# Column lists made tile by tile, 130 listed blocks for 146, and hub edge sums moved to the third layer, in a four-layer graph kernel

## The chip, the cores and the metric

The kernel runs as one program on one core of a Trainium2 chip. The time is device microseconds of one execution. The kernel before took 2622.95 us, the median of 3 runs (2618.31 to 2624.23).

## What is computed

`x` is 4096 x 256, `adj` is 4096 x 4096 in float32, with a full diagonal and otherwise few entries, many of them in the first rows and columns, few in the late ones. Four layers each add their result to `x` and normalize each row:

```python
x = layernorm(x + adj @ (x * W))                       # layer 0
x = layernorm(x + L1(x, adj, W1, W2, W3, U1, U2))       # layer 1: two steps of top-p attention and of R = (adj + I) / rowsum
x = layernorm(x + softmax_of_edges(adj, x @ H_v) @ x)   # layer 2
x = layernorm(x + [x, adj @ x, edge] @ weight + bias)   # layer 3, edge[i] = sum_j adj[i, j] * adj[j, i]
```

## The kernel before, in words

The 4096 rows are 32 tiles of 128. `adj` is cut into 32 x 32 blocks of 128 x 128. The first `DENSE` = 3 tiles of rows (the hubs) use all 32 blocks of columns in every layer. A later tile needs only the columns in which one of its rows has an entry, and these are listed: the list holds `CAPS[I]` blocks of 128 column numbers, and one block is fetched with an indirect DMA on GpSimd (`gather`, L393), which takes one index for each partition. Two index tables are kept, `idx_x` for rows of a feature table and `idx_a` for rows of the packed adjacency. `CAPS` sums to 146 over the 29 listed tiles.

**Layer 0** is a hand-written loop (L620 to L641, under `manual_schedule`, so the order of the loop is the order on PE, ACT, DVE and POOL). One round of it takes one step of several generators:

- `dense_0` (L544): tiles 0 to 15, one panel of four blocks in a round (128 rounds): a 256 KB load on SP's queue, four matmuls, and a maximum over the panel on DVE (L552) that writes into `seen` which columns have entries.
- `find_0` (L555): tiles 16 to 31 are not multiplied densely. One 512 KB load in a round, and a DVE maximum (L563); 64 rounds, so it ends halfway through the dense tiles.
- `list_columns(1)` (L319), only after `find_0` is done: the lists of tiles 16 to 31 all at once. Ten rounds of `max` and `match_replace` on DVE (L347, L349) take out eight entries each; then small matmuls and DVE steps turn them into indices.
- `listed_0` (L566), after that, one started every third round: gathers of a tile's blocks and of its rows of `x` (L393), matmuls (L593), the sum of products with the transposed block (`edge`, L595, L402, L598), a write of the gathered blocks to HBM (`packed`, L602).
- `edges_0` (L604), from the same point on: the edge sums of the three hub tiles. Two 2 MB loads of `hubs` for each tile on ACT's queue (L608) into the two `e` buffers, and two products of 2048 columns on DVE (L614).
- `list_columns(0)`: the lists of tiles 3 to 15; three steps of it at the end of layer 0, the rest beside layer 1.
- `out_0` (L477): the end of a tile, in seven steps in successive rounds: scale, normalize (with a power on POOL, L492), transpose (L245), two projections (L294, L297), a product with 512 columns (L464), copies on ACT (L299 to L304, L511), `qp` on DVE (L516), and seven stores on ACT's queue.

**Layer 1, first attention step** (L1361 on): each tile is cut into named pieces (`AT`) with times, `PERIOD` = 15.8 us apart, and the pieces of all tiles are sorted by due time. `r_stream` fetches the listed blocks of tiles 16 to 31 and 3 to 15 at evenly spaced times beside them. The remaining steps of `list_columns(0)` are further events in the first three periods. The constants that build a list from marks (`before`, `up_to`, `next_one`, `step_up`, `slots`, `slot_1`, `ranks`; L1095 to L1115) are made here. `r_dense` (L1457) then handles the three hubs, and the second attention step follows, one tile in some 32 us.

**Layers 2 and 3** are `product` (L1612) with n = 0 and n = 1. Their chunks are hub panels (`HUBS` = 3 tiles densely in layer 2, 6 in layer 3) and pieces of lists of up to five blocks, in an order with a lead of 5 and 12 hub chunks. For each kind four chunks are fetched ahead. In layer 2 each block is weighted before its matmul: an exponential on ACT (L1593), a mask on DVE (L1594); a finished tile goes through `out_2`. Layer 3's gathers read what `out_2` has stored.

Of the kernel before, what the change touches and what calls it, by code (L numbers as in the profile page):

```python
# [47 lines left out]
L_EVERY, L_WAIT = 3, 5  # L48
HB = 8
# [12 lines left out]
NL = 8  # L62
NG = 2
LE = P // NL
DENSE = 3
CAPS = (NT,) * DENSE + (7, 7, 6, 7, 5, 6, 5, 5, 5, 5, 5, 5, 6) + (5,) * 8 + (4,) * 8
PIECE = 5

# [6 lines left out]
def gnn_kernel(ctx: ExitStack, tc: tile.TileContext, x, pair, panels, W0, W1, W2T, W3T, U1T, U2T,  # L75
# [41 lines left out]
    enter(loads=6, gat=16, tmp=1, w0=2)  # L117
# [53 lines left out]
    iota16 = iota([LE], "iota16", [[1, LE]])  # L171
    place = iota([512], "place", [[1, 512]], base=1, pool=pools["tmp"])
# [3 lines left out]
    def bits(op, v, name):  # L176

        i = small.tile([P, 1], I32, name="bits")
        nc.vector.tensor_scalar(i, row, v, None, op0=op)
        t = const.tile([P, 1], F32, name=name)  # L180
        nc.vector.tensor_copy(t, i)
        return t

    def equal(iot, v, n, name, dtype=F32):
        t = const.tile([P, n], dtype, name=name)
        nc.vector.tensor_scalar(t, iot, v, None, op0=OP.is_equal)
        return t

    row_list = equal(iota8, bits(OP.bitwise_and, NL - 1, "r7"), NL, "row_list")
    row_place = equal(iota16, bits(OP.arith_shift_right, 3, "r3"), LE, "row_place", BF16)  # L190
    slot_list = bits(OP.arith_shift_right, 4, "slot_list")
    slot_is = equal(iota8, slot_list, NL, "slot_is")
    slot_tile = equal(iota16, bits(OP.bitwise_and, 15, "r15"), LE, "slot_tile")

# [117 lines left out]
    deepest = max(CAPS[DENSE:LE]), max(CAPS[LE:])  # L312
    first_col = [0, LE * deepest[0]]
    n_cols = first_col[1] + LE * deepest[1]
    idx_x = const.tile([P, n_cols], I32, name="idx_x")
    idx_a = const.tile([P, n_cols], I32, name="idx_a")
    over = const.tile([1, NG], F32, name="over")

    def list_columns(g, apart=False):  # L319

        K = deepest[g]
        n = K * LE
        own = tmp_tile([P, NT, NL, LE], BF16)
        some = pools["tmp"].tile([P, NT, LE], BF16, name="some")
        nc.vector.tensor_scalar(some, seen[:, :, g * LE:(g + 1) * LE], 0.0, None, op0=OP.is_gt)
        for s in range(NL):
            nc.vector.tensor_scalar(own[:, :, s, :], some, row_list[:, s:s + 1], None, op0=OP.mult)
        yield  # L330
        ps = bank([P, NT, LE], "psl", "tp")
        for J in range(NT):
            nc.tensor.matmul(ps[:, J, :], own[:, J].rearrange("p a b -> p (a b)"), row_place, start=True, stop=True)
        yield
        left = pools["lists"].tile([P, 512], F32, name="left")
        flat = ps.rearrange("p a b -> p (a b)")
        free = pools["lists"].tile([P, 512], F32, name="free")
        nc.vector.scalar_tensor_tensor(free, flat, 0.5, place, op0=OP.is_lt, op1=OP.mult)
        spare = one("spare")
        nc.vector.tensor_reduce(spare, free, AX.X, OP.max)  # L340
        count = one("count")
        nc.vector.tensor_reduce(count, flat, AX.X, OP.add)
        nc.vector.scalar_tensor_tensor(left, flat, 0.5, place, op0=OP.is_gt, op1=OP.mult)
        found = pools["lists"].tile([P, LE * max(deepest)], F32, name="found")
        for r in range(n // 8):
            t8 = found[:, r * 8:(r + 1) * 8]
            nc.vector.max(t8, left)  # L347
            if r < n // 8 - 1:
                nc.vector.match_replace(left, t8, left, 0.0)  # L349
            yield  # L350
        pad = free[:, :n]
        nc.vector.tensor_scalar(pad, found[:, :n], 0.0, spare, op0=OP.is_equal, op1=OP.mult)
        nc.vector.tensor_tensor(found[:, :n], found[:, :n], pad, op=OP.add)
        psi = bank([P, K, LE], "psi", "tp")
        for k in range(K):
            sel = pools["lists"].tile([P, NL, LE], F32, name="sel", bufs=2)
            fk = found[:, k * LE:(k + 1) * LE]
            nc.vector.tensor_tensor(sel, slot_is.unsqueeze(2).to_broadcast([P, NL, LE]),
                                    fk.unsqueeze(1).to_broadcast([P, NL, LE]), op=OP.mult)
            nc.tensor.matmul(psi[:, k, :], sel.rearrange("p a b -> p (a b)"), slot_tile, start=True, stop=True)  # L360
        if apart:
            yield

        cols = slice(first_col[g], first_col[g] + K * LE)
        j = free[:, :n]
        nc.vector.tensor_scalar(j, psi.rearrange("p a b -> p (a b)"), float(NL), slot_list, op0=OP.mult, op1=OP.add)
        nc.vector.tensor_scalar(j, j, float(-NL), None, op0=OP.add)
        nc.vector.tensor_copy(idx_x[:, cols], j)
        at = iota([K, LE], "at", [[0, K], [1, LE]], base=g * LE, pool=pools["lists"])
        nc.vector.scalar_tensor_tensor(idx_a[:, cols], j, float(NT), at.rearrange("p a b -> p (a b)"),  # L370
                                       op0=OP.mult, op1=OP.add)

        pst = bank([P, P], "pst", "tp")
        nc.tensor.matmul(pst[:1, :], count, ident, start=True, stop=True)
        room = pools["lists"].tile([1, NL, LE], F32, name="room")
        for i in range(LE):
            nc.gpsimd.memset(room[:, :, i:i + 1], float(CAPS[g * LE + i] * LE))
        rm = room.rearrange("p a b -> p (a b)")
        nc.vector.tensor_tensor(rm, pst[:1, :], rm, op=OP.is_gt)
        nc.vector.tensor_reduce(over[:, g:g + 1], rm, AX.X, OP.max)  # L380
# [7 lines left out]
    def col(I, k):  # L388
        c = first_col[I // LE] + k * LE + I % LE
        return slice(c, c + 1)  # L390
# [76 lines left out]
    def find_columns(J):  # L467

        for u in range(2 * J, 2 * J + 2):
            b, h = LE + u % LE, u // LE  # L470
            t = pools["loads"].tile([P, HB, P], F32, name="half", bufs=2)
            nc.sync.dma_start(t.rearrange("p (c k) i -> p c (k i)", k=JC),
                              panels[b, h * HB // JC:(h + 1) * HB // JC].rearrange("c p k i -> p c (k i)"))
            nc.vector.tensor_reduce(seen[:, h * HB:(h + 1) * HB, b], t, AX.X, OP.max, apply_absolute_value=True)

# [57 lines left out]
    def move_ends():  # L533

        far = done
        for e in ends:
            if far - e[1] >= 2:
                e[1] = e[1] + 1 if next(e[0], e) is not e else done
            far = e[1]
        while ends and ends[0][1] == done:  # L540
            ends.pop(0)
# [13 lines left out]
    def find_0():  # L555
        for b in range(LE, NT):
            e = pools["e"].tile([P, N], F32, name="e")
            for h in range(NT // HB):
                t = e[:, h * HB * P:(h + 1) * HB * P]
                nc.sync.dma_start(t.rearrange("p (c x) -> p c x", x=JC * P),  # L560
                                  panels[b, h * HB // JC:(h + 1) * HB // JC].rearrange("c p k i -> p c (k i)"))
                yield
                nc.vector.tensor_reduce(seen[:, h * HB:(h + 1) * HB, b], t.rearrange("p (t i) -> p t i", i=P), AX.X,  # L563
                                        OP.max, apply_absolute_value=True)
# [39 lines left out]
    def edges_0():  # L604
        for I in range(DENSE):
            pair_of = [pools["e"].tile([P, N], F32, name="e") for _ in range(2)]
            for t, src in zip(pair_of, hubs):
                nc.scalar.dma_start(t, src[rows(I), :])  # L608
            for _ in range(6):
                yield  # L610
            part = small.tile([P, 2], F32, name="part_e")
            for h in range(2):
                a, b = (t[:, h * (N // 2):(h + 1) * (N // 2)] for t in pair_of)
                nc.vector.scalar_tensor_tensor(a, a, 1.0, b, op0=OP.mult, op1=OP.mult, accum_out=part[:, h:h + 1])  # L614
                yield
            nc.vector.tensor_add(edge[:, I:I + 1], part[:, 0:1], part[:, 1:2])

    everything = {getattr(mybir.EngineType, k) for k in ("PE", "Activation", "DVE", "Pool")}
    with tc.manual_schedule(engines=everything):
        sums_of_edges = edges_0()  # L620
        dense = (step for I in range(LE) for step in dense_0(I))
        find, lists, others = find_0(), list_columns(1, True), None
        left, active, n, heads = list(range(LE, NT)), [], 0, 3
        while heads or ends or active or left:
            move_ends()
# [766 lines left out]
    def r_stream(blocks):  # L1392
        due, t = [], 0
        for b in blocks:
            if b == DENSE:
                run(lists)
# [458 lines left out]
```

## Time and profile before

| | us |
|---|---|
| median of the runs | 2622.95 |
| profiled execution, its own time | 2627.68 |
| its span, from the first to the last instruction | 2625.9 |
| first matmul of layer 1 (end of layer 0) | 503.8 |
| first and last `mid` (one for each tile) of the first attention step | 521.5 and 1023.9 |
| last store of layer 1, first gather of layer 2 | 2240.0, 2242.7 |
| first and last gather of layer 3 | 2455.1, 2613.8 |

PE is busy for 2197.5 us (84%), DVE 2064.5 (79%), POOL 1704.6 (65%), ACT 1478.7 (56%). The mean granted clock of TensorE is 0.933. In answers by stretch, each row gives the length, each engine's busy time and instructions, the granted clock, the share of time in which the 16 DMA engines were busy, and what they moved. In lines of the timeline the bracket is the idle time before the instruction and what ended it. In lines of waits the numbers are us in total, times, and the longest. Neither an engine's own share nor a wait says by itself what a stage is bound by: it is read from who waits last in that stage.

### The profile page before, as it was taken

How to read it: one execution, taken by the hardware profiler on the slowest of the kernel's cores; microseconds unless marked ns; L12 is line 12 of the kernel's file. 1: busy time of each engine (PE TensorE's matmuls, PEld its weight loads, DVE VectorE, ACT ScalarE, POOL GpSimd, SP SyncE). 2: the span in 40 equal slices, each digit the busy share in tenths (PEclk: the TensorE clock that was granted, in tenths of full speed). 3: DMA queues.
4: the chain of work that ended last, by engine and by line, in shares of the span. 5: the costliest groups of instructions: out<-in, count | busy, mean ns of one | idle time of the engine just before them, and what ended most of it. 6: DMA issues, size and time to landing. Idle time of an engine off the chain costs nothing.

```text
span 2625.9 us, 37696 instructions
## 1 busy us (share of the span) xinstructions
PE 2197.5 (84%) x10680; PEld 1572.6 (60%) x10680; DVE 2064.5 (79%) x6152; ACT 1478.7 (56%) x2413; POOL 1704.6 (65%) x2778
## 2 busy tenths in 40 slices
PE   6887789679988988869888888888888877798997
PEld 4666567336555555557666666666666666566774
DVE  5876455588899987366698999999999996677586
ACT  0000111258778877556688888888888982444100
POOL 1005877356666666524688888888888873677576
PEclk8999899779999989889999999999999998899997
DMA  9996977435545554635311111111111112777794
GB/s 311 350 313 224 322 229 226 131 117 165 159 139 150 149 143 140 209 116 178 111 56 49 57 47 45 53 50 48 48 47 44 54 36 77 237 227 223 238 300 156
DMA packets 261978, 392.17 MB, mean 149 GB/s; under 512 B 41920, under 2 KB 170320, under 8 KB 260992
## 3 DMA queue, kind: packets, MB, share of 16 engines
q1 hardware_dynamic: 160992, 203.82, 24.2%
q0 software_dynamic: 46112, 131.50, 17.3%
q10 hardware_dynamic: 54656, 54.35, 6.1%
q8 instruction: 88, 1.44, 0.2%
q14 instruction: 130, 1.06, 0.1%
HBM read 329.25 MB, written 60.26 MB: 148 GB/s over the span
## 4 chain that ended last, share of the span: by engine, by line
DVE 22%; PE 18%; POOL 7%; ACT 5%; issue 4%; DMA 2%; SPq 0%; POOLq 0%; DVEq 0%; ACTq 0%
PE psa L237 5%; PE acc L1659 5%; DVE cand L868 4%; DVE tmp L862 3%; PE acc L1087 2%; DVE e L914 2%; DVE top L845 2%; PE lg L671 2%; DVE rest L847 2%; ACT junk L781 2%; PE po L464 1%; POOL xg L393 1%; PE pt L226 1%; DVE e L910 1%; POOL shift L1015 1%
## 5 line engine op out<-in xcount | busy, mean ns | idle before, releaser
L237 PE MATMUL psa<-v,eT 128*128 128x256 f32 x2048 | 515.7, 400 | 81.6 <-ACT eT L228 81.6
L237 PEld LDWEIGHTS psa<-v,eT 128*128 128x128 f32 x2048 | 402.1, 200 | 162.8 <-ACT eT L228 105.9
L550 PE MATMUL acc<-xw,panel 128*128 128x257 f32 x1024 | 255.3, 399 | 38.7 <-DMA panel<-in_panels 25.7
L781 ACT ACTIVATE junk<-e,h 128x4096 bf16<-128x4096 f32 x64 | 237.4, 3710 | 52.1 <-POOL h L761 41.1
L550 PEld LDWEIGHTS acc<-xw,panel 128*128 128x128 f32 x1024 | 197.1, 199 | 96.6 <-issue 35.1
L226 PE MATMUL pt<-ident,e 128*128 128x128 f32 x1024 | 156.9, 283 | 90.4 <-DVE e L914 68.7
L787 ACT ACTIVATE junk<-e,h 128x4096 bf16<-128x4096 f32 x62 | 230.9, 3724 | 0.1
L226 PEld LDWEIGHTS pt<-ident,e 128*128 128x128 f32 x1024 | 129.7, 147 | 134.5 <-issue 82.5
L868 DVE MAX8 cand<-tmp 128x8 f32<-128x128 f32 x1024 | 203.8, 276 | 1.1
L248 ACT COPY xT<-ptx 128x256 f32<-128x256 f32 x96 | 35.8, 372 | 287.9 <-PE ptx L245 237.1
L228 ACT COPY eT<-pt 128x512 f32<-128x512 f32 x256 | 145.2, 591 | 90.5 <-PE pt L226 89.9
L393 POOL DMA_INDIRECT xg<-qtab,idx_x x146 | 140.1, 960 | 70.7 <-issue 32.5
L393 POOL DMA_INDIRECT pc<-in_pair,idx_a x146 | 150.8, 1033 | 50.1 <-issue 34.9
L393 POOL DMA_INDIRECT xg<-ttab,idx_x x146 | 145.1, 994 | 57.0 <-issue 28.5
L1167 DVE MAX8 cand<-e 128x8 f32<-128x256 f32 x512 | 175.9, 410 | 3.4 <-ACT e L1159 3.4
L393 POOL DMA_INDIRECT xg<-x2d,idx_x x146 | 147.1, 1007 | 46.7 <-issue 22.0
L1197 ACT ACTIVATE marks<-e,mid 128x1024 bf16<-128x1024 f32 x128 | 140.2, 1144 | 48.9 <-DVE mid L1193 40.8
L393 POOL DMA_INDIRECT xg<-y3d,idx_x x126 | 121.5, 964 | 59.2 <-DMA t3d<-t 21.1
L910 DVE SCALAR_TENSOR_TENSOR e<-e,ties 128x1024 f32<-128x1024 f32 x128 | 155.9, 1280 | 2.9
L1156 PE MATMUL lg<-kT,qi 64*128 64x512 f32 x512 | 154.7, 676 | 1.3 <-DVE qp L516 1.0
L464 PE MATMUL po<-u,xT 128*128 128x512 f32 x256 | 138.6, 669 | 20.3 <-DVE qp L516 19.8
L742 ACT ACTIVATE e<-lg 128x1024 f32<-128x1024 f32 x120 | 123.5, 1029 | 52.5 <-PE lg L671 52.5
(347 smaller groups left out, 5519.0 us busy)
## 6 DMA issues: line engine op xcount, KB each, us to landing
panel<-in_panels SPq DMA_DIRECT2D x200, 256.0 KB
e<-in_panels SPq DMA_DIRECT2D x64, 512.0 KB
pc<-pk SPq DMA_DIRECT2D x53, 320.0 KB
e<-in_hubs ACTq DMA_DIRECT2D x6, 2048.0 KB
xg<-ttab SPq DMA_DIRECT2D x96, 128.0 KB
pc<-pk SPq DMA_DIRECT2D x39, 256.0 KB
pc<-in_panels SPq DMA_DIRECT2D x32, 256.0 KB
tab<-xi ACTq DMA_DIRECT2D x33, 160.0 KB
```

The source lines that it names most:

```text
L226: nc.tensor.transpose(pt[:, k, :], e[:, (g * 4 + k) * P:][:, :P], ident)
L228: nc.scalar.copy(eT[g], pt)
L237: nc.tensor.matmul(ps[:, :D], eT[g][:, k, :], rhs[j][:, :D], start=(j == 0), stop=stop and j == NT - 1)
L393: nc.gpsimd.indirect_dma_start(out=o, out_offset=None, in_=src, in_offset=bass.IndirectOffsetOnAxis(ap=idx[:, c], axis=0))
L464: nc.tensor.matmul(po.rearrange("p a b -> p (a b)"), xT[:, h, :], u[:, h, :], start=(h == 0), stop=(h == 1))
L550: nc.tensor.matmul(ps[:, :D + 1], a[:, k, :], XW[j][:, :D + 1], start=(j == 0), stop=(j == NT - 1))
L781: nc.scalar.activation(junk_tile(), e, AF.Relu, bias=h, scale=-1.0, accum_out=part)
L787: nc.scalar.activation(junk_tile(), e, AF.Sign, bias=h, scale=-1.0, accum_out=below)
L868: nc.vector.max(cand[:, c * (NS // 2) + g, :], w[:, g * SEG:(g + 1) * SEG])
L910: nc.vector.scalar_tensor_tensor(eg, eg, ties[:, g:g + 1], eg, op0=OP.is_gt, op1=OP.mult)
L1156: nc.tensor.matmul(a["lg", c][:, k, :], a["qi"][r, :], kT[r, c * LC:(c + 1) * LC], start=True, stop=True)
L1167: nc.vector.max(a["cand"][:, b, :], a["e"][:, b * SEG0:(b + 1) * SEG0])
```

## The change

1. `list_columns` goes, and with it all that it needs. `list_one(I)` makes the list of one tile, exactly, from `seen[:, :, I]`, in five steps in successive rounds: prefix sums over the tiles on DVE, four small bfloat16 matmuls, two ACT copies, a comparison with `slots` on DVE, one matmul for each block, and ten small DVE steps. A list is started at most every third round, as soon as a tile's `seen` is complete; the tiles of `find_0` go first.
2. The loop of layer 0 takes one dense panel in each round, as before, but a `find_0` step in only 4 rounds of 7, so both end at nearly the same time. `listed_0(I)` starts when the list of I is made. `move_ends` keeps neighbouring tiles' ends three steps apart, for two.
3. The lists of tiles 3 to 15 are made in the same loop; layer 1 has no list events any more.
4. `CAPS` sums to 130 for 146: 64 for 72 in tiles 16 to 31, 66 for 74 in tiles 3 to 15 (111 for 126 from tile 6 on). Four tiles are in two pieces, for six.
5. `edges_0` becomes `edges_1` in layer 2: twelve pairs of 512 KB loads on SP's queue into the second half of `kT`, and twelve products of 1024 columns on DVE, one half step in each of the first 24 chunks.
6. The constants for lists are made at the start of the program, and the check at the end (`failed`) uses the lists' exact lengths: some ten small DVE steps.

```diff
-CAPS = (NT,) * DENSE + (7, 7, 6, 7, 5, 6, 5, 5, 5, 5, 5, 5, 6) + (5,) * 8 + (4,) * 8
+CAPS = (NT,) * DENSE + (7, 6, 6, 6) + (5,) * 5 + (4,) * 20
+F_SLOTS, APART = (4, 7), 3
...
+    def list_one(I):
+        K, pool = CAPS[I], pools["lists"]
+        has = pool.tile([P, NT], F32, name="has", bufs=2)
+        nc.vector.tensor_scalar(has, seen[:, :, I], 0.0, None, op0=OP.is_gt)
+        upto = pool.tile([P, NT], BF16, name="upto", bufs=2)
+        nc.vector.tensor_tensor_scan(upto, ones.to_broadcast([P, NT]), has, 0.0, op0=OP.mult, op1=OP.add)
+        nc.vector.tensor_mul(ranks[I % 2][:, :NT], upto, has)
+        mine = upto[:, NT - 1:]
+        yield
...
+        nc.tensor.matmul(pd[:, NT + 1:NT + 2], next_one, mine, start=True, stop=True)
+        nc.tensor.matmul(pd[:, NT + 2:NT + 3], before, mine, start=True, stop=True)
+        nc.tensor.matmul(pd[:, NT + 3:], up_to, mine, start=True, stop=True)
+        nc.tensor.matmul(pd[:, :NT + 1], step_up, ranks[I % 2], start=True, stop=True)
+        nc.scalar.copy(rows_of[:, I, :], pd[:, NT + 2:])
...
+        nc.scalar.copy(step, pd[:, :NT + 2])
+        yield
...
+        nc.vector.tensor_scalar(since[:, :K * P], slots[:, :K * P], rows_of[:, I, 0:1], None, op0=OP.is_ge)
+        yield
...
+        for k in range(K):
+            nc.tensor.matmul(pi[:, k, :NT + 2], since[:, k * P:(k + 1) * P], step, start=True, stop=True)
+        yield
...
+        nc.vector.tensor_sub(want, slot_1[:, :K], pi[:, :K, NT + 1])
+        nc.vector.tensor_reduce(most, ranked, AX.X, OP.max)
+        nc.vector.tensor_tensor(most, want, most, op=OP.is_le)
+        nc.vector.tensor_mul(want, want, most)
+        nc.vector.tensor_tensor(is_it, ranked, want.unsqueeze(2).to_broadcast([P, K, NT]), op=OP.is_equal)
+        nc.vector.tensor_tensor(is_it, is_it, list_base.unsqueeze(1).to_broadcast([P, K, NT]), op=OP.mult)
+        nc.vector.tensor_reduce(most, is_it, AX.X, OP.max)
...
+        nc.vector.scalar_tensor_tensor(want, most, -1.0, pi[:, :K, NT], op0=OP.add, op1=OP.add)
+        nc.vector.tensor_copy(idx_x[:, cols], want)
+        nc.vector.tensor_scalar(idx_a[:, cols], want, float(NT), float(I), op0=OP.mult, op1=OP.add)
...
     with tc.manual_schedule(engines=everything):
...
+        while multiplying or finding or soon or later or active or listing or ends:
             move_ends()
+            if n % (NT // 2 // LE) == 0:
+                multiplying = next(dense, dense) is not dense
+            if finding and (found * F_SLOTS[1] <= n * F_SLOTS[0] or not multiplying):
+                finding = next(find, find) is not find
+                found += 1
             run_rest()
+            for g in list(active):
+                if next(g, g) is g:
+                    active.remove(g)
+            for I, g in list(listing):
+                if next(g, g) is g:
+                    listing.remove((I, g))
+                    if I >= LE:
+                        active.append(listed_0(I))
+            if (soon or later) and n - started >= APART:
+                listing.append(((soon or later)[0], list_one((soon or later).pop(0))))
+                started = n
+            n += 1
...
+    def edges_1():
+        part = small.tile([P, DENSE, 4], F32, name="part_e", bufs=1)
+        half = [kT[:, N // 2:][:, s * CC:(s + 1) * CC] for s in range(2)]
+        for I in range(DENSE):
+            for c in range(N // CC):
+                for t, h in zip(half, hubs):
+                    nc.sync.dma_start(t, h[rows(I), c * CC:(c + 1) * CC])
+                yield
+                nc.vector.scalar_tensor_tensor(half[0], half[0], 1.0, half[1], op0=OP.mult, op1=OP.mult,
+                                               accum_out=part[:, I, c:c + 1])
+                yield
+        nc.vector.tensor_reduce(edge[:, :DENSE], part, AX.X, OP.add)
...
                 multiply(t)
                 passed[chunks[t][2] is not None] += 1
+                next(beside, None)
                 for g in before:
```

## The prediction

> **What bounds the kernel now.** I read the granted clock first (0.933), then the stretches between the stages, then the waits inside layer 0, then single instructions. The stretches:
>
> ```profile
> 0.00:190.00 190.00, 151.34 (x618) 112.66 (x619) 132.00 (x207) 11.90 (x37) 21.24 (x81) 0.96 0.98 333
> 190.00:230.00 40.00, 36.51 (x201) 29.79 (x200) 34.77 (x84) 2.96 (x10) 7.79 (x27) 1.00 0.58 187
> 230.00:480.00 250.00, 200.42 (x847) 151.52 (x845) 125.06 (x262) 32.03 (x116) 188.31 (x275) 0.88 0.78 245
> 480.00:504.00 24.00, 14.24 (x71) 7.67 (x72) 14.53 (x36) 4.23 (x15) 3.20 (x6) 0.72 0.45 136
> 504.00:600.00 96.00, 70.50 (x381) 36.68 (x382) 82.50 (x302) 51.84 (x88) 50.89 (x71) 0.79 0.40 121
> 600.00:1040.00 440.00, 399.69 (x2695) 244.64 (x2694) 387.16 (x1469) 349.72 (x677) 297.77 (x306) 0.96 0.53 151
> ...
> 2241.00:2455.00 214.00, 189.34 (x724) 134.19 (x725) 157.80 (x541) 95.55 (x306) 147.06 (x146) 0.96 0.73 223
> 2455.00:2626.00 171.00, 146.44 (x596) 114.40 (x594) 124.14 (x453) 0.00 (x0) 121.48 (x126) 0.90 0.74 238
> ```
>
> Columns: stretch, length, then busy time of PE, weight loads, DVE, ACT, POOL, then clock, DMA share, GB/s. Layer 0 is the first four rows and has three characters. To 190 the DMA engines are full (0.98) while `find_0` and half of the dense panels are loaded. To 230 the list of sixteen tiles is made and the DMA engines drop to 0.58. To 480 nothing is full: PE 0.80 at a clock of 0.88, POOL 0.75, DMA 0.78, DVE 0.50. Its 516 dense matmul instructions before 190 are 64.5 rounds, 2.9 us each; the 383 after 230 are 48 rounds, 5.2 us each. What keeps the last rounds long is seen in the waits of PE and, in the second fence, of ACT:
>
> ```profile
> PE po L464 <- DVE qp L516: 18.2, 7, 6.2
> PE acc L593 <- DMA xg<-in_x,idx_x: 11.6, 4, 8.3
> ```
>
> ```profile
> ACT qs L511 <- DMA tab<-xi: 14.6, 6, 3.5
> ACT qs L511 <- DMA e<-in_hubs: 12.4, 1, 12.4
> ```
>
> ACT issues the 2 MB hub loads in order with its copies, stands behind them and behind its own stores, and `qp` and the next product on PE come late. In the first attention step PE (0.91) and DVE (0.88) are both nearly full. In the two last layers the gathers follow one another without a gap:
>
> ```profile
> 2455.14 0.95 POOL L393 DMA_INDIRECT xg<-y3d,idx_x  x1 [21.12 <-DMA t3d<-t]
> 2456.39 0.94 POOL L393 DMA_INDIRECT xg<-y3d,idx_x  x1 [0.30 <-issue]
> 2457.65 0.95 POOL L393 DMA_INDIRECT xg<-y3d,idx_x  x1 [0.31 <-issue]
> ```
>
> One each 1.26 us, 126 of them from 2455.1 to 2613.8. That is layer 3's bound, and layer 2's as well (2242.7 to 2433.1 for 146, 1.31 each).
>
> **Layer 0, what it must do after the change.** DVE is busy for 306.4 us to 504. Edge sums leave (L614 and its sums, 15), lists leave (24 instructions of L347 and L349 form 17, the masks 5, the 512-wide steps 6, the rest 4: 32), eight blocks fewer of edge products save 3. Added are 29 lists. From the narrow lists of layer 1: marks, scan and rank 0.17 + 0.22 + 0.19; the comparison 0.545 for 640 columns, so some 0.44 for 512; then ten steps, of which four on 128 columns at 0.26 to 0.27 (0.32 there on 160) and six small ones at 0.16: 2.0. With 0.04 between instructions this is 3.5 us a list, 103 for all, 106 with the wider ones. Constants add 2. Sum: 306 - 15 - 32 - 3 + 108 = 364.
>
> PE at full clock, from starts in a row (16 panel instructions in 3.47 us, so 0.217): panels 1024 x 0.217 = 222, listed 128 x 0.217 = 28, 32 ends at 0.22 + 0.52 + 0.40 + 1.77 = 93, edges 2, lists 29 x 0.4 = 12 (four matmuls 0.12, five more 0.28 in layer 1). Sum 358, at a clock of 0.95 377.
>
> DMA: 0.82 x 504 = 413 us full. The hubs' 12.6 MB leave at 351 GB/s (344 at 0.98 between 30 and 180): 36. Eight blocks with 320 KB each at 245 / 0.78: 8. Left 369. POOL: 64 blocks with two gathers at 1.3, some 190 with the rest, no bound.
>
> So three resources need 364 to 377 us each and the layer, 504 long, uses them one after another today. The change lays them side by side: gathers begin beside the loads, the 40 us of lists without loads are gone, the hub loads no longer stand before ACT's copies. What it pays with is coupling: a list crosses from DVE to PE to ACT to DVE to PE to DVE, one round for each crossing, on engines that work in order. Behind a list matmul that waits stand the next panel's four matmuls; behind the comparison stand the panel maximum, which frees the load buffers, and the next tile's end. Bounds: if the fullest resource reaches 0.98 as the DMA engines do to 190, a round is 377 / 0.98 / 128 = 3.0 us; if nothing is gained from the overlap beyond the lost list stretch and the hub stall, the rounds keep today's mean (480 / 128 = 3.75). I take 0.90, as PE holds in the first attention step with the same kind of lists beside it (0.91): 377 / 0.90 = 419, with 8 for the start (first data) and 13 for the last tile's chain (24 today, with 8 us of list steps in it and a second tile): 440 for 504, **-64** (ends: -99 and -3).
>
> Here a rule speaks against the change. The row first:
>
> ```profile
> L1236 DVE TENSOR_SCALAR since<-slots,listed x32: 542/545/745, 536.6 to 1039.8; 128x640 bf16<-128x640 f32 x32
> ```
>
> ```profile
> L495 DVE TENSOR_SCALAR xi<-y,mv,rs x32: 402/412/952, 47.5 to 487.8; 128x256 f32<-128x256 f32 x32
> ```
>
> (minimum, median, maximum in ns). The Trainium skill ("SBUF — State Buffer", Who interferes with whom) says that a `tensor_scalar` on VectorE can take the port pair that it shares with GpSimd, for the whole instruction, and that whichever starts second is blocked until the other is done. The list steps of that kind now run beside gathers. By the rule each of 29 comparisons and 29 marks could stand behind a gather of 0.95 us: 55 us of DVE, which would then be the bound (419 of 440). By the row, beside 306 POOL instructions, the median is 3 ns above the minimum and the worst is 0.2 above it; L495 shows that a doubling happens, rarely. I take the row: 1 us.
>
> **First attention step.** Between 504 and 620 leave 12 of L347 (8.1), 11 of L349 (8.4), seven selections (1.8), some 2 of small steps and 2 of constants: 22 of DVE, which is busy 82.5 of 96 there. The first `mid` would come 5 earlier, and the periods of the first five tiles sum to 90.1 where five at the later mean of 15.86 are 79.3: 11. That is 16 of the 22; the rest DVE must share with PE and ACT, so 14. The 16 blocks fewer are 16 x 0.43 = 7 us of PE over 32 periods in which DVE is as full: 1. **-15** (ends -6, -22).
>
> **Second attention step.** 16 blocks fewer beside a DVE at 0.87 and a chain of DVE, ACT and POOL: **-2** (0 to -6).
>
> **Layer 2.** 16 gathers fewer at 1.31: -21 if gathers stay the bound. Against it stand the 12.6 MB of hubs. DMA share times length is 0.73 x 214 = 156; minus 3.1 MB (10) plus 36 to 41: 184 in what would be 193. But the loads lie in the first 24 of 57 chunks; after the lead of five such chunks take some 3.2 us each today. Two of them carry 1.45 MB (6.3 us at 230 GB/s) and the pair of loads 1.05 MB; at 315 GB/s, between 223 / 0.73 = 305 and the 351 above, that is 7.9 us. Eleven pairs at +1.6: +17. The first pair is loaded before layer 2 begins, so it costs nothing; the second comes with the panels and holds DVE, behind it the mask L1594 and PE: +4. DVE's own 12 x 1.25 = 15 fit in its idle quarter. Sum **0** (ends -21: hidden; +18: DVE held for 3 us more at each pair).
>
> **Layer 3.** 15 gathers fewer at 1.26: -19. PE is at 0.96 between 2460 and 2580 and the DMA engines at 0.87, so with the same hub panels in less time something else is next: PE has 83 + 48 = 131 us, gathers 140, so they stay last. I keep 3 back for the fuller DMA engines: **-16** (-10 to -19). The small steps of the final check (some 3 us of DVE) can run before the end.
>
> Sum: -64 - 15 - 2 + 0 - 16 = -97. The profiled execution took 2627.7, so 2531; the median of the runs lies 4.7 below it: **2526 us**.
>
> **Rivals.** (a) The overlap is as good as the loads of today's first part: rounds of 3.0 us, layer 0 at 405 (-99), hub loads half hidden (-10), the rest -35: some 2480. For it: 0.98 to 190. Against: there DVE was at 0.69, now near 0.9. (b) Rounds stay at 3.75: layer 0 at 501, the rest -33, some 2587. For it: DVE, PE and DMA all near full in lockstep. (c) Slower: PE stands in layer 0 at lists. 29 lists make it wait twice, for the marks and for the comparison; if DVE lags by its work of one round (364 / 128 = 2.8), that is 58 x 2.8 = 165 us; 377 + 21 + 165 = 563, and with -33 elsewhere 2649. It decides from (504 + 33 - 398) / 58 = 2.4 us a wait. Against: PE's longest sum of waits on DVE in the first attention step, which has 32 such lists, is 7.4 us over 8 waits. (d) It does not do what it says: gathers are delayed until the loads end, and nothing changes.
>
> **How the numbers follow.** Forecast 0.48 (its own range 2500 to 2556), (a) 0.21, (b) 0.22, (c) 0.06, (d) 0.03. Range 2480 to 2590: it takes in the middle of (a) and nearly all of (b). Faster by over 0.2%, about what a measurement can tell from no change: 0.91; within 0.03; slower 0.06.
>
> **What would show it.** The first matmul of layer 1 at about 440 (405, 501, 563 for the rivals); the DMA share at about 0.85 throughout layer 0, with no stretch like that at 190; the first five periods near 15.9; layer 2's gathers with gaps in its first 24 chunks and its length unchanged; 111 gathers at 1.26 in layer 3. I am wrong if DVE's waits for PE or PE's for list steps exceed 40 us in layer 0, or if the twelve hub products hold DVE for over 40.

## The result, and the profile after

The changed kernel takes 2589.49 us (median of 4 runs, 2581.96 to 2592.77) where the kernel before took 2620.63 on the same chip: a ratio of 0.9876, 95% interval 0.985 to 0.9902. So it is 1.2% faster, by 31 us, where 97 were forecast. The total lies just inside the stated range (2480 to 2590), but that is luck: layer 0 came out above both of its ends, and the first attention step made up for a part of it. The profiled execution took 2589.5 us, its span is 2587.7. The stages of the two profiled executions, from one landmark to the next (first matmul of layer 1, last `mid`, first gathers of layers 2 and 3, end):

| stage | before | after | change | forecast |
|---|---|---|---|---|
| layer 0 | 503.8 | 511.9 | +8 | -64 |
| first attention step | 520.1 | 480.0 | -40 | -15 |
| hubs and second attention step | 1218.8 | 1208.6 | -10 | -2 |
| layer 2 | 212.4 | 228.5 | +16 | 0 |
| layer 3 | 170.8 | 158.7 | -12 | -16 |

The same stretches after, columns as in the prediction:

```profile
0.00:190.00 190.00, 151.22 (x665) 112.92 (x666) 121.62 (x295) 17.91 (x69) 71.54 (x155) 0.93 0.83 273
190.00:230.00 40.00, 30.08 (x142) 22.43 (x140) 25.81 (x67) 4.97 (x21) 15.69 (x25) 0.91 0.71 241
230.00:480.00 250.00, 207.92 (x982) 158.74 (x983) 181.13 (x487) 29.25 (x122) 107.05 (x167) 0.91 0.70 220
480.00:512.00 32.00, 23.18 (x101) 15.82 (x98) 16.49 (x52) 6.20 (x24) 3.44 (x6) 0.84 0.40 134
...
2198.00:2410.00 212.00, 174.71 (x623) 121.39 (x624) 158.71 (x528) 87.72 (x283) 135.46 (x130) 0.90 0.81 252
2410.00:2588.00 178.00, 147.27 (x635) 121.98 (x633) 134.53 (x489) 2.61 (x7) 106.43 (x111) 0.92 0.71 227
```

The three characters of layer 0 are gone: it is one even stretch now, a round takes some 3.9 us from 90 to 500 us (2.6 until 213 us and 5.3 from 231 us on before, by the panel maxima of DVE). But nothing is full in it. To 512 us PE is busy for 412, DVE for 345, POOL for 198, and the DMA share is 0.73, where some 0.85 were forecast:

```profile
0.00:512.00 512.00, 412.40 (x1884) 309.90 (x1884) 345.05 (x898) 58.34 (x236) 197.72 (x351) 0.91 0.73 236
```

What the engines wait for, over layer 0 after (us in total, times, longest):

```profile
PE psq L292 <- ACT xT L246: 24.6, 11, 6.1
...
PE lists_ps L329 <- DVE want L356: 15.5, 7, 4.6
PE lists_ps L329 <- DVE upto L324: 14.3, 4, 4.3
PE lists_ps L342 <- DVE since L338: 8.4, 7, 2.7
...
DVE qp L485 <- ACT qs L480: 90.9, 29, 8.8
...
ACT rows_of L333 <- PE lists_ps L332: 113.1, 24, 8.4
```

PE waits 38.2 us for list steps (L329 and L342), DVE 91 us for ACT, ACT 113 us for the lists' matmuls. One of PE's waits from near. First the timeline of PE after, with the idle time and what ended it in the bracket:

```profile
289.93 1.90 PE L519 MATMUL acc<-xw,panel 128*128 128x257 f32 x8
294.97 0.16 PE L329 MATMUL lists_ps<-upto,next_one 128*128 128x1 bf16 x1 [3.14 <-DVE want L356]
...
296.82 3.73 PE L442 MATMUL po<-u,xT 128*128 128x512 f32 x4
```

The timeline of DVE after, at the same time:

```profile
292.23 0.19 DVE L325 TENSOR_TENSOR ranks<-upto,has 128x32 bf16<-128x32 bf16 x1
...
294.76 0.16 DVE L356 SCALAR_TENSOR_TENSOR want<-most,lists_ps 128x4 f32<-128x4 f32 x1
```

And the stretches of 5 us after (the clock is the third number from the end):

```profile
290.00:295.00 5.00, 1.86 (x11) 1.39 (x10) 4.55 (x20) 0.53 (x2) 1.52 (x3) 0.97 0.85 296
295.00:300.00 5.00, 5.00 (x16) 3.27 (x16) 4.42 (x8) 0.98 (x5) 3.19 (x3) 0.50 0.40 120
300.00:305.00 5.00, 5.00 (x26) 3.93 (x25) 1.14 (x3) 0.74 (x2) 4.36 (x8) 0.85 0.94 242
```

The first list matmul needs the marks, made by 292.4. PE starts it at 294.97, just when DVE has read the list before out of the same PSUM tile (L356 ends at 294.92). DVE was busy nearly all that time, with the end of a tile, a maximum and that list. And this wait costs twice: for the next 5 us the granted clock is 0.50, and four matmuls of `po` take 3.73 us that take 1.94 us at 305.7.

Eleven of the runs below, marked *, were on chips on which the kernel before itself takes 2968 to 3000 us (in the traces from these chips, which are of changed kernels, the engines stand for times that are put down to no other engine, most of it in the first attention step), so they are compared with one another and not with the rest. The ends of stages below are read from one profiled execution of each run; a few us between two of them say nothing.

### The profile page after: what moved, and what is told of

It reads as the page before. It is cut to its first block, busy times and chain, and to the rows that moved or that the text cites. A ratio compares the mean times of both kernels' runs of the same rounds, so it can differ in the third digit from the quotient of the medians.

```text
span 2587.7 us, 37783 instructions
## 1 busy us (share of the span) xinstructions
PE 2152.6 (83%) x10692; PEld 1548.5 (60%) x10692; DVE 2093.1 (81%) x6433; ACT 1478.8 (57%) x2455; POOL 1603.6 (62%) x2648
## 4 chain that ended last, share of the span: by engine, by line
DVE 32%; PE 12%; ACT 5%; issue 4%; POOL 3%; DMA 3%; SPq 0%; DVEq 0%; ACTq 0%; POOLq 0%
DVE cand L830 5%; DVE e L876 4%; DVE tmp L824 4%; PE psa L235 3%; DVE e L872 3%; PE acc L1621 2%; PE acc L1059 2%; DVE top L807 2%; DVE rest L809 2%; DMA kT<-in_hubs 2%; DVE vt L267 1%; ACT junk L743 1%; PE lg L633 1%; PE pt L224 1%; DVE rs L268 1%
## 5 line engine op out<-in xcount | busy, mean ns | idle before, releaser
L235 PE MATMUL psa<-v,eT 128*128 128x256 f32 x2048 | 505.1, 393 | 75.5 <-ACT eT L226 75.3
L235 PEld LDWEIGHTS psa<-v,eT 128*128 128x128 f32 x2048 | 395.1, 197 | 150.3 <-ACT eT L226 96.1
L519 PE MATMUL acc<-xw,panel 128*128 128x257 f32 x1024 | 264.5, 406 | 16.0 <-DMA xw<-in_x 15.8
L371 POOL DMA_INDIRECT pc<-in_pair,idx_a x130 | 128.2, 986 | 95.4 <-issue 44.3
L371 POOL DMA_INDIRECT xg<-x2d,idx_x x130 | 135.5, 1042 | 65.1 <-PE acc L1621 27.1
L371 POOL DMA_INDIRECT xg<-ttab,idx_x x130 | 129.1, 993 | 54.9 <-issue 28.1
L371 POOL DMA_INDIRECT xg<-qtab,idx_x x130 | 124.3, 956 | 54.0 <-issue 28.7
L824 DVE SCALAR_TENSOR_TENSOR tmp<-e,h 128x2048 f32<-128x2048 f32 x64 | 150.5, 2352 | 2.3
L633 PE MATMUL lg<-kT,qi 64*128 64x512 f32 x480 | 135.5, 641 | 17.5 <-ACT junk L707 17.4
L1109 PE MATMUL lg<-kT,qi 64*128 64x512 f32 x512 | 147.0, 650 | 3.0 <-DVE want L356 2.8
L371 POOL DMA_INDIRECT xg<-y3d,idx_x x111 | 106.4, 959 | 64.2 <-DMA t3d<-t 30.6
```

Of the source, the lines that this page charges most:

```text
L235: nc.tensor.matmul(ps[:, :D], eT[g][:, k, :], rhs[j][:, :D], start=(j == 0), stop=stop and j == NT - 1)
L371: nc.gpsimd.indirect_dma_start(out=o, out_offset=None, in_=src, in_offset=bass.IndirectOffsetOnAxis(ap=idx[:, c], axis=0))
L519: nc.tensor.matmul(ps[:, :D + 1], a[:, k, :], XW[j][:, :D + 1], start=(j == 0), stop=(j == NT - 1))
L633: nc.tensor.matmul(ps[:, h, :], qi[r, :], kT[r, (n * NC + c) * LC:][:, :LC], start=True, stop=True)
L824: nc.vector.scalar_tensor_tensor(w, ec, h, ec, op0=OP.is_lt, op1=OP.mult, accum_out=low[:, c:c + 1])
L1109: nc.tensor.matmul(a["lg", c][:, k, :], a["qi"][r, :], kT[r, c * LC:(c + 1) * LC], start=True, stop=True)
```

## The experiments

**The lists left out.** `list_one` is replaced by empty steps, the indices by constants, so other columns are gathered; behind layer 3 the kernel's `failed` branch then computes everything without lists (22369 us in all), and only layer 0 is read.

```diff
     def list_one(I):
-        ...
+        for _ in range(4):
+            yield
...
+            nc.gpsimd.iota(idx_x[:, c:c + 1], [[1, 1]], base=k * P, channel_multiplier=1)
```

> The changed kernel with the work of the column lists left out of layer 0: the indices are constants (columns p + 128 k), written by GpSimd before the loop, so the gathered columns are other ones; the order of rounds, loads, gathers and matmuls stays. Theory C (DVE's and PE's summed work sets the round): DVE loses some 100 us of 345 and PE 12; rounds fall to some 3.2 us, layer 0 ends at 430, total some 2507. Theory A (hand-offs): the same end or a little later, 430 to 450, but the waits of PE for list steps (38 us, plus the slow matmuls after them) are what goes. Theory B (ACT's order at qs): only the list's two copies leave ACT, layer 0 stays above 490, total above 2567.

Layer 0 ends at 426.0. Its row, 0 to 426:

```profile
0.00:426.00 426.00, 369.46 (x1638) 281.27 (x1638) 260.34 (x493) 51.29 (x178) 215.48 (x611) 0.98 0.86 283
```

So the lists cost 86 us of layer 0. DVE's wait for `qs` is 94.5 us here, as long as with the lists, and PE is still at 0.87 at a clock of 0.98: so that wait is not what holds the layer at 512, and theory B falls as the main cause. A and C are told apart by the next two.

**DVE's part alone, and all parts with none handed on.** In the first the lists' matmuls and copies are left out. In the second all are there, but PE's matmuls and DVE's steps read constants; ACT's two copies still read what the matmuls wrote. Indices are constants in both, so the gathers read other columns, and none waits for a list.

```diff
-        nc.tensor.matmul(pi[:, k, :NT + 2], since[:, k * P:(k + 1) * P], step, start=True, stop=True)
+        nc.tensor.matmul(pi[:, k, :NT + 2], ident_bf, step_up[:, :NT + 2], start=True, stop=True)
...
-        ranked = pi[:, :K, :NT]
+        ranked = still[:, :K, :NT]
```

> DVE's part of the lists alone, a second time (its matmuls and copies left out, constant indices). The first time layer 0 ended at 454, on a chip where engines also stood for some us with nothing that they waited for. Against 426 without lists and 512 with them: if amounts are what costs, this run takes the larger part of the 86, ends at 470 or above; if hand-offs do, 430 to 450.

> All instructions of the lists on DVE, PE and ACT, none handed on, a second time (constant indices). The first time layer 0 ended at 484, on a chip where ACT stood some 45 us with nothing that it waited for. If hand-offs are 40 us or more of the 86: 470 or less. If the amount of instructions on PE and ACT costs as much as DVE's: 480 to 490.

Layer 0 ends at 446.8 and at 471.9 (454 and 484 in the first measurements*). The row of the first:

```profile
0.00:447.00 447.00, 376.34 (x1638) 289.59 (x1640) 347.49 (x900) 51.30 (x178) 216.38 (x611) 0.96 0.83 270
```

The row of the second:

```profile
0.00:472.00 472.00, 392.33 (x1884) 301.55 (x1886) 346.68 (x893) 58.07 (x236) 216.86 (x611) 0.95 0.78 256
```

The 87 us of work on DVE cost 21. The instructions on PE and ACT cost another 25, of which 16 are PE's own busy time (392 - 376). The last 40 (512 - 472) come when the steps are handed on; in them is also that the gathers read the true columns and wait for their lists. So both theories hold in part: 46 for amounts, 40 for hand-offs. The hand-off from PE to ACT is in the 25 and not in the 40, since it was still there (ACT stood 82 us at these copies for PE in the second run). In the prediction's terms: PE's busy time goes from 369 to 412, some 16 for the lists' matmuls and the rest by the clock, which falls from 0.98 to 0.91; PE's idle time goes from 57 to 100.

**Lists four rounds apart.**

```diff
-F_SLOTS, APART = (4, 7), 3
+F_SLOTS, APART = (4, 7), 4
```

> The changed kernel with lists started four rounds apart for three; nothing else. With three, the first small matmuls of a list stand in the same round as the last DVE steps of the list before it, which read the same PSUM tile, so PE waits for DVE inside one round (15.5 us over 7 waits in the changed kernel, and slower matmuls for some us after each). Theory A (hand-offs between PE and DVE with no slack set the round): this wait goes, layer 0 ends at some 480 instead of 512, total some 2560. Theory B (ACT's order: DVE stands for qs): waits only move, layer 0 at 505 to 515, total 2585 to 2595. Theory C (PE and DVE have so much work that rounds are 4.0 us anyway): the same as B.

2565.83 us, ratio 0.9795 (0.977 to 0.9821). Layer 0 ends at 486.8, 25 us earlier; nothing else moves by more than 2, and the medians of the whole kernel differ by 23.7. PE's and DVE's waits in layer 0:

```profile
PE lists_ps L329 <- DVE upto L324: 19.2, 10, 4.6
...
DVE qp L485 <- ACT qs L480: 59.5, 25, 7.7
```

Its row, 0 to 486:

```profile
0.00:486.00 486.00, 397.50 (x1882) 295.59 (x1882) 342.88 (x894) 58.69 (x236) 198.24 (x351) 0.94 0.77 249
```

The wait for `want` is gone, and the clock is 0.94 for 0.91. Five steps in five rounds and a start three rounds after the list before put the next list's first matmuls into the round in which the list before is read from the same tile: a hand-off with no slack at all. By DVE's panel maxima, 11 of the 28 starts came three rounds after the one before; with four, none can. The last list still starts at the last round, so the lists are not merely spread over more rounds. That one place was 25 us, with all that follows from its waits. A second PSUM tile in turn, which would remove it without moving a list, was not tried.

**`qs` first on ACT.**

```diff
+        nc.scalar.copy(qs, po[:, 1, :])
         run(qk)
         nc.scalar.dma_start(tab[rows(I), :], xi)
...
-        nc.scalar.copy(qs, po[:, 1, :])
```

> The changed kernel with the copy of qs moved ahead of the copies of kT, q and xi and of the four stores on ACT; nothing else. In the changed kernel DVE stands at qp for qs, 91 us over 29 waits, and behind qp stand the panel maxima that free load buffers. Theory B (ACT's order sets the round): most of the 91 us go and layer 0 ends 30 us or more earlier, at 480 or below, total some 2560 or less. Theory A (hand-offs of the lists) and theory C (sum of work): the 91 us shrink but DVE then waits elsewhere, for PE or for loads, and layer 0 ends at 500 to 512, total 2577 to 2592.

2578.74 us, ratio 0.9831 (0.9803 to 0.9858). DVE's wait for `qs` falls from 91 to 54.5 us, layer 0 ends at 502.2, 10 earlier. A gain, but a third of what theory B wanted.

**More slack, or one crossing fewer.** All with lists four rounds apart. One round more between marks and matmuls (first alone*, then twice with the edit of layer 2 below*); the two copies of a list by DVE for ACT*; and `qs` first*.

```diff
         mine = upto[:, NT - 1:]
         yield
+        yield
```

```diff
-        nc.scalar.copy(rows_of[:, I, :], pd[:, NT + 2:])
+        yield
+        nc.vector.tensor_copy(rows_of[:, I, :], pd[:, NT + 2:])
...
-        nc.scalar.copy(step, pd[:, :NT + 2])
-        yield
+        nc.vector.tensor_copy(step, pd[:, :NT + 2])
```

> Lists four rounds apart as in the run with 2565.8 us, and the four small matmuls of a list one round later than its marks (one more yield), so that DVE has two rounds for them. In the run with four rounds apart PE still waits 19.2 us over 10 waits for the marks, with slower matmuls after each, and layer 0 ends at 487. Theory A (PE and DVE wait for each other at hand-offs without slack): layer 0 ends at 465 to 475, total some 2548 to 2556. Theory C (the amount of work of DVE and PE): 483 to 490, total 2562 to 2570.

> Lists four rounds apart, the copy of qs ahead of ACT's other copies and stores, and the hub products of layer 2 three chunks behind their loads. Layer 0: 512 with neither, 487 and 502 with one of the two; if they act on different waits 477, if on the same ones 487. Layer 2 as in the run with the later matmuls. Total 2535 to 2550 with the layer 2 gain, 2556 to 2566 without.

> As the run before it in this list, with the four small matmuls of a list one round later. With all list instructions kept and none handed on, layer 0 ended at 472; so hand-offs are 40 of the 86 us, and four rounds apart took 25 of them. Theory A (slack is what is missing): 472 to 480 in layer 0, total 2540 to 2549. If the remaining 15 are the gathers' later start and not waits of PE: 485 to 495, total 2550 to 2562; on slower chips it was 497 and 503.

> As the first run of this list, with the two small copies of a list made by DVE, ahead of its comparison, for ACT. In the changed kernel ACT stands 113 us at these copies for PE. It takes one crossing away, and adds 29 times some 0.35 us to DVE (10 us). If ACT's place in the chain costs more than that: layer 0 at 470 to 480, total 2538 to 2548. If DVE's amount is what counts (21 us of layer 0 for 87 us more on DVE, so 2.5 us for 10): 487 to 492, total 2550 to 2560.

On the stalling chips layer 0 ends at 495.9 with four rounds apart alone, at 503.1, 496.8 and 505.1 with the later matmuls, at 490.5 with DVE's copies and at 515.9 with `qs` first. The same code differs by 8 us there, so only this is said: more slack for the marks gains nothing (PE's wait for the marks goes, but in the third run with it 19.3 us at `xi` and 16.1 at `since` stand in its place, 10.6 and 8.4 without it), one crossing fewer is worth at most some 5, and no gain of `qs` first on top of the other edit is seen (its profiled execution was 13 us above the median of its runs). So the 15 us between 487 and 472 stay unexplained.

**Hub edges left out, and their products later.** First the three hubs' edge sums are left out (set to 0). Then they are kept, with each product three chunks behind its loads for one.

```diff
                     nc.sync.dma_start(t, h[rows(I), c * CC:(c + 1) * CC])
                 yield
+                yield
+                yield
```

> The changed kernel with the edge sums of the three hub tiles left out altogether (set to 0): no 12.6 MB of hub loads and no twelve products in layer 2. The third layer took 228.5 us from its first gather to the first gather of the fourth, against 212.4 before with 16 gathers more. If hub loads cost what the prediction said (some 21 us in the third layer, of which 17 for loads), it falls to some 207, total 2568. If they are hidden, it stays at 222 or more, total 2583 or more. If they hold DVE and, behind it, PE and the gathers, it falls to 192 (the 130 gathers at 1.31 us and the last tile's chain), total 2553.

> The changed kernel with the hub products of layer 2 three chunks behind their loads for one, so over 48 chunks for 24. Without the hub edges the third layer took 202.6 us, with them 228.5. DVE waited 23.5 us over 8 waits for these loads. If the price is DVE standing for loads that take longer than one chunk, and behind it the masks, PE and the gathers: 205 to 210, total 2567 to 2573. If the price is the DMA engines' time in the first chunks: the same total bytes over twice the chunks, 215 to 222. If it is DVE's and the queue's work itself: 225 or more, total above 2585.

Without them: 2563.44 us, ratio 0.9785 (0.9759 to 0.981), layer 2 in 202.6. So they cost 26 us. The gathers of layer 2 in the changed kernel (minimum, median and maximum in ns, first and last start):

```profile
L371 POOL DMA_INDIRECT xg<-x2d,idx_x x130: 943/949/1861, 2200.5 to 2397.5; - x130
```

The same without hub edges:

```profile
L371 POOL DMA_INDIRECT xg<-x2d,idx_x x130: 940/946/1442, 2200.2 to 2371.3; - x130
```

And the last stretch of layer 2 without hub edges:

```profile
2320.00:2398.00 78.00, 72.77 (x277) 49.83 (x276) 62.73 (x224) 32.12 (x103) 37.75 (x38) 0.98 0.71 209
```

Without hub edges the 130 gathers take 171 us (1.32 each), 19 less than the 146 before. But layer 3's first gather comes 31.5 us after the last of them, for 22.0 before: PE is at 0.93 over the last 78 us. So I read layer 2 as bound by PE once the gathers are fewer: PE is busy for 184 us of it for 189 before, and the layer is 10 us shorter, not 19.

With the later products, on a stalling chip*, layer 2 takes 242.4, where the same chip took 253.7 with the products one chunk behind. DVE's waits for these loads are gone, which were in layer 2 of the changed kernel:

```profile
DVE kT L1569 <- DMA kT<-in_hubs: 23.5, 8, 7.2
```

That took off only 11 us, for 26 that the edges cost on the other chips. Where the rest goes is argued, not shown: the bytes are still loaded. The first 60 us of layer 2 in the changed kernel, and the same without hub edges:

```profile
2200.00:2260.00 60.00, 42.39 (x137) 31.24 (x138) 36.24 (x105) 21.27 (x68) 46.53 (x43) 0.78 0.92 301
```

```profile
2200.00:2260.00 60.00, 52.16 (x193) 38.16 (x194) 41.22 (x137) 29.55 (x96) 45.76 (x47) 0.91 0.79 232
```

With the edges the DMA engines are at 0.92 there for 0.79, and PE at 0.71 for 0.87.

**146 blocks in the changed kernel.** The capacities of the kernel before, nothing else.

```diff
-CAPS = (NT,) * DENSE + (7, 6, 6, 6) + (5,) * 5 + (4,) * 20
+CAPS = (NT,) * DENSE + (7, 7, 6, 7, 5, 6, 5, 5, 5, 5, 5, 5, 6) + (5,) * 8 + (4,) * 8
```

> 146 listed blocks in the changed kernel, for its stages on a chip on which the kernel before takes some 2622. First attention step 480 to 485 if the lists that left it are the whole cause of the 40 us, 492 or more if the 16 blocks are a good part. Layer 0 at 530 (twice 532 to 534 elsewhere, 20 more than with 130 blocks), layer 2 at 235 to 250, layer 3 at 176.

2665.89 us in one run, beside 2622.01 for the kernel before (elsewhere*: ratios 1.0059, 1.0043 to 1.0075, and 1.0042, 1.0028 to 1.0057). Layer 0 ends at 536.3, the first attention step takes 499.5, the part to layer 2 1216.6, layer 2 239.8, layer 3 171.9. So 16 blocks fewer are worth 76 us in this run: 24 in layer 0, 20 in the first attention step, 8 behind it, 11 in layer 2, 13 in layer 3. Without them the change is slower than the kernel before in all three measurements: all that it gains, it gains by the shorter lists.

**Together.** Lists four rounds apart and the later hub products*.

> The two edits that helped alone, together: lists four rounds apart, and the hub products of layer 2 three chunks behind their loads. Layer 0 at 487, first attention step 466 to 480 long, layer 2 at 212 to 216 (228.5 with the products one chunk behind, 202.6 without edges; on a slower chip the same edit took 13 off), total 2550 to 2556. If the gain in layer 2 is not there on this chip: 2563 to 2568.

2895.18 us, ratio 0.9651 (0.9615 to 0.9686), with the best of the kernels that leave nothing out. The changed kernel's own 0.9876 is from a chip without the stalls, so the two ratios can't be set side by side. With DVE's copies it is 0.965 (0.9621 to 0.9678), with the later matmuls 0.9666 (0.964 to 0.9692) and 0.9661 (0.9619 to 0.9703), which these intervals don't tell apart; with `qs` first 0.9683 (0.9648 to 0.9719), and the later hub products alone 0.9763 (0.9735 to 0.9792).

## Why the prediction was wrong

**Layer 0 (forecast -64, ends -99 and -3, measured +8).** The step that failed is "I take 0.90, as PE holds in the first attention step with the same kind of lists beside it". That the three resources lie side by side is right, and the amounts were near: DVE is busy for 345 us (364 forecast, which counts gaps between the list steps), and the lists add 87 us to it (103 forecast, with the gaps). Without lists the layer does end at 426. But with them PE is at 0.81 at a clock of 0.91, 412 us of 512, not at 0.90 at 0.95 with 377. The first attention step was no measure for it: there the pieces of a list are sorted by due time, here each crossing has one round, and the list tile's next use had none where lists started three rounds apart. The prediction named the coupling ("a list crosses from DVE to PE to ACT to DVE to PE to DVE, one round for each crossing, on engines that work in order") and priced it with a share from another stage. It did not work out in which round the next list writes the tile that the list before is still read from; that alone was 25 us. The other 61 of the lists' 86 are 21 for DVE's added work, 25 for the instructions on PE and ACT, and 15 that stay open, by the counts above. The other miss in this step is the clock: 0.95 was taken without a reason (over all of layer 0 it was 0.91 before too), and 0.91 came out, for 0.98 without lists. So the waits also make PE's work longer: of the 43 us by which PE's busy time grew with the lists, some 27 are the clock's.

**Its own marks.** "I am wrong if DVE's waits for PE or PE's for list steps exceed 40 us": PE waits 38.2 for list steps, DVE 33 for PE. The hub products stood 23.5 us for their loads, for 40. The marks were not reached and the forecast was wrong all the same: the recorded waits leave out the slow matmuls behind them, and what the lists' own work costs.

**The rivals.** (b) gave 2587, and its end of layer 0 (501) is nearest, but not its reason: nothing is near full. (c) is the mechanism that acted in part, at less than a quarter of its size: 18 recorded waits of PE at lists, 2.1 us each, 38 us in all, for 58 of 2.8, 165 us.

**The rule on the shared port.** The 1 us was right in size, but for a reason that the row of the comparisons could not show. The comparisons and the marks after:

```profile
L338 DVE TENSOR_SCALAR since<-slots,rows_of x29: 454/478/676, 45.3 to 502.5; 128x512 bf16<-128x512 f32 x20, 128x640 bf16<-128x640 f32 x5, 128x768 bf16<-128x768 f32 x3, 128x896 bf16<-128x896 f32 x1
L322 DVE TENSOR_SCALAR has<-seen x29: 152/178/426, 42.1 to 501.4; 128x32 f32<-128x32 bf16 x29
```

The comparisons are not stretched: those of 512 columns take 455 to 478 ns beside a gather, one of them wholly inside a gather, and 454 to 486 but for one of 582 without. The marks are: none of the 15 without a gather takes over 179 ns, but 10 of the 14 beside one take 206 to 426. That is some 1 us in all, far from the 55 us of the rule.

**First attention step (-15, measured -40).** The lists' part was mis-sized a little (-14; -21 in the run with 146 blocks), the blocks' part grossly: "16 x 0.43 = 7 us of PE over 32 periods in which DVE is as full: 1" was 20. It was costed as PE's matmuls; each block also takes one gather or two on POOL's queue, in order before the gathers that the attention waits for. 24 gathers at 1.26 are 30 us of POOL; that this is the cause is argued, not shown, and it is not known for the 8 us behind it either (forecast 2).

**Layer 2 (0, measured +16).** Two terms. "16 gathers fewer at 1.31: -21 if gathers stay the bound" failed: they did not stay it, PE's work came next by the reading above, and the gain is 10. The hub edges were forecast at +21 (17 + 4) and cost 26.

**Layer 3 (-16, measured -12)** lies within its ends; the 13 from blocks, less 1 for the rest.

## What to carry to other kernels

Where steps on several in-order engines are laid side by side, list every hand-off with the rounds between the write and the read, including the next turn's write into a tile that is still being read; a hand-off with no round of slack can cost its wait and slow matmuls after it. Don't carry a share of busy time from one stage to another that is ordered differently. When two resources are near each other, take the second one's time as the floor before a gain on the first is booked.

## What was not expected of the hardware

After a wait of PE of 3.1 us, the clock record has 0.50 from 294.72 to 301.54, and four matmuls took 3.73 us for 1.94. Over layer 0 it has 18 such stretches, of 3.4 to 10.2 us and 89 us together; without lists 4, with 14 us. The kernel before has 13, with 92 us, so half the clock is not new in layer 0. The Trainium skill ("TensorE: Matmul & The Clock Gate", The HAM clock gate) says that after an idle window of about 3.4 us the array goes to half its rate, and that about as long a window of sustained work brings it back. The trace agrees in kind and not in length: PE had no work from 291.83 to 294.97 alone, and the full clock came back 6.6 us after its work did.

Whole chips differ: on three chips the kernel before took 2968 to 3000 us for 2622 on the others. The cause stays open. An instruction of ACT takes the same time there (the exponential of L1112 1024 ns in the median on both). On one of them, the stretch from first to last `mid` took 711 us for 467, with ACT and DVE busy for as long as elsewhere (377 and 439 us for 379 and 432), PE at a clock of 0.79 for 0.97, and waits that the trace puts down to no engine. Also open is why eight gathered blocks fewer shorten layer 0 by 24 us where their matmuls, gathers and bytes come to 8 at most by the prediction's count.
